# First unit's keys by token tile, Wk on ScalarE's queue, and four pieces of work in other slots, in an attention and expert layer

## The chip, the cores and the metric

The kernel runs on one core of one Trainium2 chip. The metric is the device time of one execution in microseconds (us), as the median of several runs. The profile shows one more execution, recorded by the hardware profiler. The engines are PE (TensorE, matmuls), PEld (its weight loads), DVE (VectorE), ACT (ScalarE), POOL (GpSimd) and SP (SyncE, which issues most of the DMAs). Each takes its instructions in the order in which they were issued to it.

## The reference

The input x has 2 batches of 512 tokens with 512 features, all in float32. The layer is

```python
q, k, v = x @ Wq + bq, x @ Wk + bk, x @ Wv + bv     # 32 query heads, 8 key/value heads, head size 128
q, k = rope(q), rope(k)
ctx = softmax(causal(q k^T / sqrt(128))) v           # four query heads share a key/value head
x = layernorm(x + ctx @ Wo + bo)
z = x @ lora_A[active]^T                             # 4 active experts, rank 8
alpha = softmax(log(prior) + x @ router_W^T + router_b)   # over the active experts
y = x @ W_base^T + b_base + sum_e alpha_e * 2 * (z_e @ lora_B[e]^T)
out = layernorm(x + y)
```

## The kernel before, in words

A unit is one key/value head of one batch: its four query heads against its own keys, 16 units in all. A unit has 16 score blocks ("slots") of 32 queries x 4 heads = 128 rows. The order of all instructions is written out by hand (`tc.manual_schedule()`): a function `slot(T)` issues what belongs to slot T, for T from -8 on, and `put(T, f)` hangs further work at the end of a slot. In slot T, TensorE gets query products, key or value products, output products, the score of block T and the context products of an older part; then ScalarE and VectorE get the exponentials, sums and transposes of blocks T-1 to T-4. A score bank in PSUM is used again two slots later, so the score of block s needs the exponential of block s-2. The probabilities are transposed through VectorE and a round trip over DRAM (`blocks_out`, `blocks_in`, on SP's queue).

**The start.** Lines 193 to 210 issue the loads: ScalarE's queue the three bias loads into `bqk`; SP's queue the four x tiles of batch 0, Wk of the first head (`load_k(0)`, line 198), Wq of two heads, the rope table, Wq of the other two, Wv, the x tiles of batch 1, and more. The DMA semaphores are eight, given out in turn to the DMAs of the two queues; an issue that uses one again waits until the DMA that had it has landed. On TensorE, lines 1048 to 1057 issue three idle matmuls, the transposes of the four tiles (`transpose_token_tile`, four 128x128 transposes into one bank and one copy, alternately on VectorE and ScalarE, line 282), the transpose `tb` of the biases (line 1054), and then the keys of unit 0: four matmuls with 512 columns, one for each 128 features (`k_mm`, line 361). After it stand the query projection of unit 0 (`q_mm`, two heads, a value tile, two heads) with `q_rope`, and `k_rope` with the rope table on VectorE.

**Wo's sums.** Most products use a seven-product scheme for 2x2 blocks. For the output projection, four VectorE operations (`wo_sums`, line 637) form sums of Wo's blocks in `wt` and in Wo itself, once for each set n of Wo. Lines 942 to 945 put them at slots relative to `wo_from(u) = 16 u + 21`. For set 0 they are at slots 21, 22, 22 and 24. The first product that reads `wt` is in slot 23.

**W_base's transposes.** In the last slots, from `T_PROJ = T_END - 19`, W_base is loaded in four chunks (line 1114, on SP's queue) and transposed (`transposed_base`, line 1111): four transposes on TensorE and a copy on ScalarE (line 282) for each chunk, at slots T_PROJ + 4, 6, 8 and 10.

**The end.** After the slots come the last token tiles of the second half by hand (lines 1137 to 1223). The objects are `f0` (tiles of batch 0), `fz = f0[3]`, `fa`, `fb`, `fc` (tiles of batch 1). `logits` and `alphas` (lines 789 to 810) do the routing: two VectorE operations, an exponential on ScalarE, and VectorE operations that end in `zs`; `low_rank` transposes `zs` into `zT` (tile `tz`, line 814, copy line 815); `finish` adds the low-rank product (line 819); `sum` adds x (line 829); `add` is `sum` and the statistics (lines 703, 704); `root` is the root on ScalarE (line 711) and the reciprocal on VectorE (line 714). The exponential and the root need different tables on ScalarE, so that table loads stand between them.

Of the kernel before, what the change touches and what calls it, by code (L numbers as in the profile page):

```python
# [9 lines left out]
F32 = mybir.dt.float32  # L10
# [5 lines left out]
P = 128  # L16
# [3 lines left out]
D = 128  # L20
# [9 lines left out]
def postln_layer_kernel(  # L30
# [33 lines left out]
    nc = tc.nc  # L64
    B, S, HID = x.shape
    NT = B * S // P
    TPB = S // P
    KC = HID // P
# [19 lines left out]
    NSETS = len(sets)  # L88

    def unit(u):  # L90
        return units[u]
# [4 lines left out]
    def set_units(n):  # L96
        return [u for u in range(NU) if set_of(u) == n]
# [8 lines left out]
    ps_q = ctx.enter_context(tc.tile_pool(name="ps_q", bufs=1, space=bass.MemoryType.PSUM))  # L106
    ps_k = ctx.enter_context(tc.tile_pool(name="ps_k", bufs=1, space=bass.MemoryType.PSUM))
    ps_sc = ctx.enter_context(tc.tile_pool(name="ps_sc", bufs=2, space=bass.MemoryType.PSUM))
# [5 lines left out]
    x_sb = const.tile([P, NT, HID], F32, name="x_sb")  # L114
# [3 lines left out]
    NBIAS = H + 2 * G  # L118
    bqkT = const.tile([P, NBIAS], F32, name="bqkT")
# [7 lines left out]
    ident = const.tile([P, P], F32, name="ident")  # L127
# [10 lines left out]
    xT = proj.tile([P, KC, B * S], F32, name="xT")  # L138
# [6 lines left out]
    wqk = {}  # L145
    wos = {}
    wvs = {}

    def load_k(g):
        wk_g = wts.tile([P, KC, D], F32, tag="wk_g", name=f"wk_{g}")  # L150
        nc.sync.dma_start(out=wk_g, in_=Wk[:, ts(g, D)].rearrange("(c p) n -> p c n", p=P))
        wqk["k", g] = wk_g

    def load_q(n, k):
        wq_g = wts.tile([P, KC, 2 * D], F32, tag="wq_g", name=f"wq_{n}_{k}", bufs=3)
        lo = (sets[n] * R + 2 * k) * D
        nc.sync.dma_start(out=wq_g, in_=Wq[:, lo : lo + 2 * D].rearrange("(c p) n -> p c n", p=P))
        wqk["q", n, k] = wq_g
# [11 lines left out]
    def load_x(t, n):  # L170
        nc.sync.dma_start(
            out=x_sb[:, t : t + n, :], in_=xf[t * P : (t + n) * P, :].rearrange("(t p) n -> p t n", p=P))


    for n in range(2):
# [6 lines left out]
        out=tri, in_=tri, pattern=[[-BLK, QB], [-1, BLK]], compare_op=ALU.is_ge,  # L182
# [6 lines left out]
    for z in zt:  # L189
        nc.gpsimd.memset(z, 0.0)  # L190

    bqk = setup.tile([NBIAS, D], F32, name="bqk")
    nc.scalar.dma_start(out=bqk[:H, :], in_=bq.rearrange("(h d) -> h d", d=D))
    nc.scalar.dma_start(out=bqk[H : H + G, :], in_=bk.rearrange("(h d) -> h d", d=D))
    nc.scalar.dma_start(out=bqk[H + G :, :], in_=bv.rearrange("(h d) -> h d", d=D))
    for t in range(TPB):
        load_x(t, 1)
    load_k(0)
    load_q(0, 0)
    nc.sync.dma_start(out=rope_sb, in_=rope[:, 2:4, :])  # L200
    load_q(0, 1)
    load_wv(0)
    load_x(TPB, 2)
    load_x(TPB + 2, 2)
    load_k(1)
    bo_bc = setup.tile([P, HID], F32, name="bo_bc")
    nc.sync.dma_start(out=bo_bc, in_=bo.partition_broadcast(P))
# [66 lines left out]
            gather(b_act[:, a, :], lora_B.rearrange("e (p j) r -> (e p) (j r)", j=BJ), idx["b"][:, a : a + 1])  # L274


    def transpose_token_tile(dst, src, pool, tag, copy):

        tp = pool.tile([P, KC, P], F32, tag=tag, name="tp")
        for c in range(KC):  # L280
            nc.tensor.transpose(tp[:, c, :], src[:, ts(c, P)], ident)  # L281
        copy(dst, tp)

    b_jar = setup.tile([P, BJ, EA, RK], F32, name="b_jar")

# [40 lines left out]
    psq = {}  # L326
    sc = {}
# [27 lines left out]
    in_psum = set()  # L355

    def proj_mm(key, pool, tag, wt, cols, b, c):
        if c == 0:
            psq[key] = pool.tile([P, S], F32, tag=tag, name="pp")
            in_psum.add(key)  # L360
        nc.tensor.matmul(  # L361
            psq[key], lhsT=wt[:, c, cols], rhs=xT[:, c, ts(b, S)], start=(c == 0), stop=(c == KC - 1))
# [22 lines left out]
    def k_mm(u, c):  # L385
        g, b = unit(u)
        proj_mm(("k", u), ps_k, "k", wqk["k", g], slice(0, D), b, c)

    def k_of(u):
        if u not in kT:  # L390
            kT[u] = work.tile([P, UNIT, BLK], F32, tag="kT", name=f"kT_{u}", bufs=5)
        return kT[u]
# [234 lines left out]
    def wo_sums(n, step):  # L627

        if step == 0:
            shape = [P, 3, CH, NHALF]  # L630
            if n == NSETS - 4:
                wt[n] = late["pool"].tile(shape, F32, name="wt_late")
            else:
                wt[n] = wow.tile(shape, F32, tag="wt", name=f"wt_{n}", bufs=1)
        t1, t2, t4 = (wt[n][:, m] for m in range(3))
        b11, b12, b21, b22 = (wo_block(n, c_half, n_half) for c_half in range(2) for n_half in range(2))
        nc.vector.tensor_tensor(
            *((t1, b12, b11), (t2, b22, t1), (b12, b22, b12), (t4, b21, t2))[step], ALU.subtract)
# [104 lines left out]
    class Ffn:  # L743
# [22 lines left out]
        def transpose(self, pool, tag):  # L766
            transpose_token_tile(self.xT, self.x, pool, tag, nc.scalar.copy)
# [107 lines left out]
    def put(slot, f):  # L875
        extra.setdefault(slot, []).append(f)

    copies = (nc.vector.tensor_copy, nc.scalar.copy)
# [39 lines left out]
    for p in range(1, G // VG):  # L918
        at = PERIOD * p
        put(13 if p == 1 else at - PERIOD + 9, lambda p=p: load_k(VG * p))  # L920
        put(37 if p == 1 else at - PERIOD + 13, lambda p=p: load_k(VG * p + 1))
        put(40 if p == 1 else at - 2 * UNIT + 3, lambda p=p: kv_sums("k", p))
        if p > 1:
            put(at - PERIOD + 37, lambda p=p: load_wv(p))
        put(at + (UNIT if p == 1 else 0) + 3, lambda p=p: kv_sums("v", p))
# [10 lines left out]
    def wo_from(u):  # L936
        return UNIT * u + LAG_WO
# [2 lines left out]
        put(wo_from(set_units(n - 2)[-1] + 1) + 1, lambda n=n: load_wo(n))  # L940

    for n in range(NSETS - 2):
        at = {NSETS - 4: (-16, -15, -15, -13), NSETS - 3: (-11, -9, -6, -5)}.get(n, (0, 1, 1, 3))
        for k in range(4):
            put(wo_from(set_units(n)[0]) + at[k], lambda n=n, k=k: wo_sums(n, k))

# [15 lines left out]
    def slot(T):  # L962
# [14 lines left out]
        if 0 < uk < PLAIN_K and l < KC:  # L977
            k_mm(uk, l)
# [66 lines left out]
    spare = ((ps_wo, "wx"), (ps_wo, "wy"), (ps_ctx, "ctx"), (ps_sc, "sc"))  # L1045
# [2 lines left out]
    idle = ps_sc.tile([P, 2 * P], F32, tag="sc", name="idle")  # L1048
    for _ in range(3):
        nc.tensor.matmul(idle, lhsT=maskw[:, :P], rhs=maskw[:, : 2 * P], start=True, stop=True)  # L1050
    for t in range(TPB):
        transpose_token_tile(xT[:, :, ts(t, P)], x_sb[:, t, :], *spare[t], copies[t % 2])
    tb = ps_sc.tile([P, NBIAS], F32, tag="sc", name="tb")
    nc.tensor.transpose(tb, bqk, ident[:NBIAS, :NBIAS])
    nc.vector.tensor_copy(bqkT, tb)
    for c in range(KC):
        k_mm(0, c)
    for part in range(3):
        k_rope(0, part)
    expert_rows()  # L1060
# [1 line left out]
    for r in range(R):  # L1062
        for c in range(KC):
            q_mm(0, r, c, *q_banks[r])
        for part in range(3):
            q_rope(0, r, part)
        if r == 2:
            for t in range(TPB, NT):
                transpose_token_tile(xT[:, :, ts(t, P)], x_sb[:, t, :], *spare[t % 2 + 2], nc.scalar.copy)
        elif r:  # L1070
            v_tile(0, r // 2, *spare[r // 2 * 2])
            v_out(0, r // 2)
# [9 lines left out]
    T_PROJ = T_END - 19  # L1082
# [15 lines left out]
    def tiles(ts_, banks, name):  # L1098
        n = len(ts_)
        norms = Norm(ffn_pool, n, f"a{name}"), Norm(ffn_pool, n, f"f{name}")  # L1100
        return [Ffn(t, bank, *norms, i) for i, (t, bank) in enumerate(zip(ts_, banks))]

    f0 = tiles(range(TPB), ((QX, QY), (QX, QY), (SC, SC), (QX, QY)), "0")
    fa = tiles([TPB + i for i in order[:2]], ((SC, SC), (WX, WY)), "1a")
# [5 lines left out]
    def transposed_base(c):  # L1110
        transpose_token_tile(wbT[:, :, c // 2, ts(c % 2, P)], wb_sb[:, c, :], ps_k, "k", nc.scalar.copy)

    for c in range(OC):
        put(T_PROJ + (0, 1, 4, 5)[c], lambda c=c: nc.sync.dma_start(out=wb_sb[:, c, :], in_=W_base[ts(c, P), :]))
        put(T_PROJ + (4, 6, 8, 10)[c], lambda c=c: transposed_base(c))
    put(A - 5, lambda: f0[0].norm1.newton(0, 2))
    for k, f in enumerate(f0):
        put(A + (-7, -6, 0, 0)[k], f.stats)
# [18 lines left out]
    fz = f0[3]  # L1137
# [17 lines left out]
    fb.centre()  # L1155
    f0[2].norm2.stats(2, f0[2].y)
    f0[0].norm2.root(0, 3)
    for f in f0[:3]:
        f.store()
    for j in range(2):  # L1160
# [2 lines left out]
    for f in fa:  # L1163
        f.transpose(*SC)
    fb.transpose(*CTX)
    fz.logits()
    fz.alphas()
    for r in range(R):
        wo_mm(NP - 1, r)
    wo_out(NP - 1)  # L1170
# [30 lines left out]
    fb.logits()  # L1201
    fb.alphas()
    fa[1].finish()
    fa[1].add()
    fa[1].norm2.sqrt(1, 2)
    for c in range(KC):
        fc.half(0, c)
    fc.half_end(0)
    fb.low_rank()
    fa[1].norm2.invert(1, 2)  # L1210
    fa[1].store()
    fc.half_stats(0)
    for c in range(KC):
# [60 lines left out]
```

## Time and profile before

| | |
|---|---|
| median of three runs | 823.33 us (822.33 to 825.24) |
| profiled execution: time | 822.99 us |
| profiled execution: span of the instructions | 821.2 us |
| busy in the span | PE 810.6, DVE 603.7, ACT 379.2, POOL 320.9 us |
| granted TensorE clock | 0.999 |

The page gives the busy time of each engine, the chain of work that ended last, the groups of instructions by line and the DMA issues. Times in it are counted from the start of the span. A float32 matmul stands in the records as two; PE's ends are modelled, so a stop of TensorE is read from the starts of successive matmuls, and from the release shown in brackets at the end of a row: how long the engine was idle before, and what ended it.

### The profile page before, as it was taken

To read this page: it belongs to the slowest core of one execution; us is meant where nothing else is said; L and a number is where in the kernel's file an instruction comes from. 1 tells how busy PE (TensorE), PEld (TensorE's weight loads), DVE (VectorE), ACT (ScalarE), POOL (GpSimd) and SP (SyncE) were. 2 spreads that over 40 slices of the span, in tenths; PEclk is the share of its full clock that TensorE was granted. 3 is DMA by queue.
4 is the path that set the end of the run, shared out by engine and by line. 5 is a ranking of instruction groups with operands and counts; after the bars stand their busy time and mean duration, and the time that the engine had idled before them with its cause. 6 is when DMAs were issued, how large, how long until landed. Compare 5 with 4: busy or idle time off the path is not lost.

```text
span 821.2 us, 11196 instructions
## 1 busy us (share of the span) xinstructions
PE 810.6 (99%) x3385; PEld 598.5 (73%) x3385; DVE 603.7 (74%) x1972; ACT 379.2 (46%) x1058; POOL 320.9 (39%) x377
## 2 busy tenths in 40 slices
PE   8999999999999999999999999999999999999996
PEld 5567777777777778777777878777777878655565
DVE  4367877677878876787868777787888689974455
ACT  1236453453545554444545444444545454663244
POOL 6464343512543545321453245343464333420033
PEclk9999999999999999999999999999999999999999
DMA  9015636445474637354454627355453726674211
GB/s 306 22 39 148 213 77 174 134 118 163 103 208 107 201 91 218 90 141 156 135 150 126 190 66 224 97 154 180 134 148 96 225 65 183 187 257 142 77 39 65
DMA packets 84415, 116.00 MB, mean 141 GB/s; under 512 B 6525, under 2 KB 64237, under 8 KB 82306
## 3 DMA queue, kind: packets, MB, share of 16 engines
q1 hardware_dynamic: 83682, 114.98, 48.7%
q8 instruction: 27, 0.44, 0.2%
q14 instruction: 34, 0.28, 0.1%
q0 software_dynamic: 448, 0.14, 0.1%
q10 hardware_dynamic: 224, 0.16, 0.1%
HBM read 71.21 MB, written 44.04 MB: 140 GB/s over the span
## 4 chain that ended last, share of the span: by engine, by line
PE 94%; DVE 3%; ACT 1%; DMA 1%; issue 0%; POOL 0%; SPq 0%; DVEq 0%; POOLq 0%
PE pc L608 16%; PE sc L552 14%; PE qx L440 12%; PE wx L440 11%; PE qy L440 9%; PE wy L440 9%; PE pp L361 5%; PE kx L440 4%; PE vx L518 4%; PE py L778 3%; PE po L684 3%; PE pv L344 3%; PE tp L281 1%; PE py L819 1%; DMA x_sb<-_attn_hidden_states_dram 1%; DVE st L703 0%
## 5 line engine op out<-in xcount | busy, mean ns | idle before, releaser
L560 DVE CUSTOM_DVE_ANT_0 sc<-sc,maskw 128x288 f32<-128x288 f32 (+15 forms) x256 | 114.2, 446 | 139.6 <-PE sc L552 138.1
L567 ACT ACTIVATE p<-sc,nmax 128x288 f32<-128x288 f32 (+15 forms) x256 | 124.3, 485 | 200.5 <-DVE nmax L560 179.0
L608 PE MATMUL pc<-pT,v 128*128 128x512 f32 x320 | 165.4, 599 | 0.0
L552 PE MATMUL sc<-kT,qT 128*128 128x160 f32 (+15 forms) x512 | 161.8, 398 | 1.0 <-ACT p L567 1.0
L382 POOL TENSOR_TENSOR qT<-q,t 128x512 f32<-128x512 f32 x56 | 76.5, 1365 | 178.8 <-DVE q L381 176.0
L575 ACT ACTIVATE p<-p,den 128x288 f32<-128x288 f32 (+15 forms) x256 | 133.2, 521 | 0.0
L552 PEld LDWEIGHTS sc<-kT,qT 128*128 128x128 f32 x512 | 96.1, 190 | 23.9 <-issue 9.8
L615 ACT ACTIVATE ctxT<-pc,bqkT 128x512 f32<-128x512 f32 x64 | 44.0, 687 | 118.0 <-PE pc L608 118.0
L427 POOL TENSOR_TENSOR cs<-ctxT 128x256 f32<-128x256 f32 x28 | 22.5, 802 | 157.7 <-PE wy L440 94.5
L583 DVE STREAM_TRANSPOSE zt<-p 128x128 f32<-128x128 f32 (+2 forms) x192 | 81.6, 425 | 0.0
L608 PEld LDWEIGHTS pc<-pT,v 128*128 128x128 f32 x320 | 57.1, 190 | 18.7 <-issue 5.7
L440 PE MATMUL qx<-xs,wq 128*128 128x256 f32 x224 | 58.0, 381 | 0.0
L476 ACT COPY q<-qx 128x256 f32<-128x256 f32 x112 | 41.4, 370 | 35.2 <-PE qx L440 35.1
L440 PEld LDWEIGHTS qx<-xs,wq 128*128 128x128 f32 x224 | 41.4, 190 | 22.2 <-issue 18.4
L440 PE MATMUL wx<-wo,ctxT 128*128 128x256 f32 x224 | 57.6, 379 | 0.0
L585 DVE STREAM_TRANSPOSE zt<-p 128x32 f32<-128x32 f32 (+3 forms) x256 | 57.5, 225 | 0.0
L567 ACT ACTIVATION_READ_ACCUMULATOR p<-sc,nmax 128x1 f32 x256 | 49.8, 195 | 0.0
L440 PEld LDWEIGHTS wx<-wo,ctxT 128*128 128x128 f32 x224 | 42.5, 190 | 7.7 <-issue 1.4
L670 DVE TENSOR_TENSOR x_sb<-wx,x_sb 128x256 f32<-128x256 f32 x112 | 47.0, 420 | 0.0
L374 DVE SCALAR_TENSOR_TENSOR t<-q,bqkT,rope_sb 64x512 f32<-64x512 f32 x56 | 45.6, 815 | 1.5
L377 DVE SCALAR_TENSOR_TENSOR t<-q,bqkT,rope_sb 64x512 f32<-64x512 f32 x56 | 42.7, 762 | 1.3
L571 DVE RECIPROCAL den<-den 128x1 f32<-128x1 f32 x256 | 39.3, 153 | 1.3 <-ACT p L567 1.2
(233 smaller groups left out, 1482.1 us busy)
## 6 DMA issues: line engine op xcount, KB each, us to landing
db<-zt SPq DMA_DIRECT2D x64, 256.0 KB, 4.2
pT<-db SPq DMA_DIRECT2D x16, 1024.0 KB, 4.8
db<-zt SPq DMA_DIRECT2D x64, 192.0 KB, 3.2
pT<-db SPq DMA_DIRECT2D x16, 768.0 KB, 4.5
wq<-in_L_attn_Wq_dram SPq DMA_DIRECT2D x20, 512.0 KB, 5.1
wo<-in_L_attn_Wo_dram SPq DMA_DIRECT2D x10, 1024.0 KB
db<-zt SPq DMA_DIRECT2D x64, 128.0 KB, 2.3
pT<-db SPq DMA_DIRECT2D x16, 512.0 KB, 4.1
```

Of the source, the lines that this page charges most:

```text
L374: nc.vector.scalar_tensor_tensor(t2[lo, :], q[hi, :], b_ap[hi, :], rope_sb[hi, 1, :], ALU.add, ALU.mult)
L382: nc.gpsimd.tensor_tensor(dst, t1[:, :].rearrange("p (n s) -> p n s", s=BLK), t2[:, :].rearrange("p (n s) -> p n s", s=BLK), ALU.add)
L440: nc.tensor.matmul(ps, lhsT=wt[:, c, :], rhs=xt[:, c, :], start=start and c == 0, stop=c == CH - 1, skip_group_check=True)
L552: nc.tensor.matmul(sc[s][:, :w], lhsT=qT[u][:, i * QB + n].rearrange("p r s -> p (r s)"), rhs=kT[u][:].rearrange("p n s -> p (n s)")[:, :w ...
L560: nc.vector.tensor_tensor_reduce(sc[s][:, :w], sc[s][:, :w], maskw[:, S - w :], -SCALE, -MASKED, ALU.add, ALU.min, nmax[s])
L567: nc.scalar.activation(ptile[s][:, :w], sc[s][:, :w], AF.Exp, bias=nmax[s], scale=-1.0, accum_out=rden[s])
L575: nc.scalar.activation(ptile[s][:, :w], ptile[s][:, :w], AF.Copy, scale=rden[s])
L583: nc.vector.transpose(z[:, :, last - i : last, n, :].rearrange("p q j s -> p j q s"), ptile[s][:, : i * P])
L585: nc.vector.transpose(z[:, : n + 1, last, n, :], ptile[s][:, i * P : w])
L608: nc.tensor.matmul(psc[p], lhsT=v_sb[g // VG, b][:, j, ts(g % VG, D)], rhs=pT[p][:, :, ts(j, P)], start=(j == 0), stop=(j == i))
L615: nc.scalar.activation(ctxT[p], psc[p], AF.Identity, bias=bqkT[:, col : col + 1])
L670: nc.vector.tensor_tensor(into, pw[k, bank], into, ALU.add)
```

## The change

Wk's first load moves to ScalarE's queue ahead of the biases. The keys of unit 0 are computed for each token tile of 128 columns (`k_tile`) instead of for 512 columns at once, each tile two steps behind its transposes; the fourth x tile is transposed into two banks with two copies; the biases' transpose moves behind the third tile. Set 0's four Wo sums go to slots 16, 17, 18 and 19. W_base's first and last transposes go one slot earlier. At the end `fz`'s routing is issued before the last context, and `fa[1]`'s statistics and root after `fb`'s copy of `zT`.

```diff
-    def load_k(g):
+    def load_k(g, queue=nc.sync):
...
-        nc.sync.dma_start(out=wk_g, in_=Wk[:, ts(g, D)].rearrange("(c p) n -> p c n", p=P))
+        queue.dma_start(out=wk_g, in_=Wk[:, ts(g, D)].rearrange("(c p) n -> p c n", p=P))
...
+    load_k(0, nc.scalar)
     bqk = setup.tile([NBIAS, D], F32, name="bqk")
...
-    load_k(0)
     load_q(0, 0)
...
-    def transpose_token_tile(dst, src, pool, tag, copy):
+    def transpose_token_tile(dst, src, pool, tag, copy, chunks=range(KC)):
-        tp = pool.tile([P, KC, P], F32, tag=tag, name="tp")
-        for c in range(KC):
-            nc.tensor.transpose(tp[:, c, :], src[:, ts(c, P)], ident)
-        copy(dst, tp)
+        tp = pool.tile([P, len(chunks), P], F32, tag=tag, name="tp")
+        for n, c in enumerate(chunks):
+            nc.tensor.transpose(tp[:, n, :], src[:, ts(c, P)], ident)
+        copy(dst[:, chunks[0] : chunks[-1] + 1, :], tp)
...
+    def k_tile(u, t, c):
+        g, b = unit(u)
+        key = "k", u
+        if t == c == 0:
+            psq[key] = ps_k.tile([P, S], F32, tag="k", name="pp")
+            in_psum.add(key)
+        nc.tensor.matmul(
+            psq[key][:, ts(t, P)], lhsT=wqk["k", g][:, c, :], rhs=xT[:, c, ts(b * TPB + t, P)],
+            start=(t == c == 0), stop=(c == KC - 1), skip_group_check=True)
...
-        at = {NSETS - 4: (-16, -15, -15, -13), NSETS - 3: (-11, -9, -6, -5)}.get(n, (0, 1, 1, 3))
+        at = {0: (-5, -4, -3, -2), NSETS - 4: (-16, -15, -15, -13), NSETS - 3: (-11, -9, -6, -5)}.get(n, (0, 1, 1, 3))
...
     for t in range(TPB):
-        transpose_token_tile(xT[:, :, ts(t, P)], x_sb[:, t, :], *spare[t], copies[t % 2])
-    tb = ps_sc.tile([P, NBIAS], F32, tag="sc", name="tb")
-    nc.tensor.transpose(tb, bqk, ident[:NBIAS, :NBIAS])
-    nc.vector.tensor_copy(bqkT, tb)
-    for c in range(KC):
-        k_mm(0, c)
+        x_to = xT[:, :, ts(t, P)], x_sb[:, t, :]
+        if t > 1:
+            for c in range(KC):
+                k_tile(0, t - 2, c)
+        if t < TPB - 1:
+            transpose_token_tile(*x_to, *spare[t], copies[t % 2])
+        else:
+            for n, bank in enumerate((spare[t], (ps_q, "qx"))):
+                transpose_token_tile(*x_to, *bank, copies[n], range(2 * n, 2 * n + 2))
+        if t == 2:
+            tb = ps_sc.tile([P, NBIAS], F32, tag="sc", name="tb")
+            nc.tensor.transpose(tb, bqk, ident[:NBIAS, :NBIAS])
+            nc.vector.tensor_copy(bqkT, tb)
+    for t in range(TPB - 2, TPB):
+        for c in range(KC):
+            k_tile(0, t, c)
...
-        put(T_PROJ + (4, 6, 8, 10)[c], lambda c=c: transposed_base(c))
+        put(T_PROJ + (3, 6, 8, 9)[c], lambda c=c: transposed_base(c))
...
     f0[0].norm2.root(0, 3)
+    fz.logits()
+    fz.alphas()
     for f in f0[:3]:
         f.store()
...
     fb.transpose(*CTX)
-    fz.logits()
-    fz.alphas()
...
     fa[1].finish()
-    fa[1].add()
-    fa[1].norm2.sqrt(1, 2)
+    fa[1].sum()
...
     fb.low_rank()
-    fa[1].norm2.invert(1, 2)
+    fa[1].norm2.stats(1, fa[1].y)
+    fa[1].norm2.root(1, 2)
     fa[1].store()
```

## The prediction

> **What bounds the kernel now.** I read the page first (busy time, chain of work that ended last), then the busy times by stage, then the places at which TensorE stops: the start, about 102 us, about 720 us and the end. Page and stages:
>
> ```profile
> PE 810.6 (99%) x3385; PEld 598.5 (73%) x3385; DVE 603.7 (74%) x1972; ACT 379.2 (46%) x1058; POOL 320.9 (39%) x377
> PEclk9999999999999999999999999999999999999999
> PE 94%; DVE 3%; ACT 1%; DMA 1%; issue 0%; POOL 0%; SPq 0%; DVEq 0%; POOLq 0%
> ...
> 0.00:8.38 8.38, 5.57 (x23) 4.09 (x24) 2.14 (x5) 2.46 (x3) 7.60 (x20) 1.00 0.75 235
> 102.00:717.00 615.00, 615.00 (x2651) 471.34 (x2652) 483.27 (x1574) 297.73 (x854) 248.84 (x281) 1.00 0.51 145
> 717.00:722.00 5.00, 4.03 (x17) 2.36 (x16) 4.03 (x18) 3.63 (x10) 2.45 (x12) 1.00 0.58 152
> ```
>
> TensorE (PE) is the bound at full clock: between 102 and 717 us it is busy in every one of 615.00 us. Matmul starts follow each other at 0.43 us per recorded 512 columns, so little but more TensorE work, or less standing still, moves the end. Three stretches have holes; the start and the 720 us stretch read so in order of time:
>
> ```profile
> 0.74 1.89 SPq L171 DMA_DIRECT2D x_sb<-_attn_hidden_states_dram  x4
> 2.67 0.45 SPq L151 DMA_DIRECT2D wk<-in_L_attn_Wk_dram  x1
> 3.43 0.37 SPq L157 DMA_DIRECT2D wq<-in_L_attn_Wq_dram  x1
> 5.79 0.66 PE L281 MATMUL tp<-ident,x_sb 128*128 128x128 f32 x4 [0.54 <-DMA x_sb<-_attn_hidden_states_dram]
> 7.05 0.66 PE L281 MATMUL tp<-ident,x_sb 128*128 128x128 f32 x4 [0.60 <-DMA x_sb<-_attn_hidden_states_dram]
> 8.38 3.70 PE L361 MATMUL pp<-xT,wk 128*128 128x512 f32 x8 [0.49 <-ACT xT L282]
> ...
> 101.33 0.59 PE L552 MATMUL sc<-kT,qT 128*128 128x256 f32 x2
> 101.98 1.13 PE L440 MATMUL qy<-xT,wq 128*128 128x256 f32 x4
> ...
> 721.30 0.91 PE L552 MATMUL sc<-kT,qT 128*128 128x384 f32 x2 [0.97 <-ACT p L567]
> ...
> 792.98 0.28 PE L814 MATMUL tz<-ident,zs 128*32 128x128 f32 x1 [0.22 <-DVE zs L805]
> ...
> 812.68 1.13 PE L819 MATMUL py<-bmT,zT 128*128 128x256 f32 x4 [0.51 <-DVE zT L815]
> ```
>
> To see: the key projection cannot start before the fourth x tile has landed (7.05) and been copied (8.38); one score at 721.30 waits for ScalarE, with its own sequence 1.13 us late; at the end two small waits remain.
>
> **Part 1, the start.** Removed: four 128x512 key matmuls at 8.38, 3.44 us until 11.82. Added: sixteen of 128 columns, four per x tile. The nearest row, eight 128x128 records at 0.89 (vx, L518), gives 4 x 0.89 = 3.56, so 0.12 us more work, but three quarters of it can be done while x arrives. The last tile's copy is split over VectorE and ScalarE (about 0.4 us each where one copy took 0.59).
>
> What it costs is in the queues. Wk goes from the fifth place on SP's queue to the first on ScalarE's, ahead of the three bias loads; the table load behind it (2.10 to 3.38) starts some 0.45 us later, and hides, because ScalarE's first copy is at 5.29. The bytes are not free: an x packet (2 KB) took 84 ns, a Wk packet (512 B) 27 ns, on 16 engines, so an x tile is 128 x 84 / 16 = 0.67 us and Wk is 512 x 27 / 16 = 0.86. Tiles three and four therefore land up to 0.86 later, near 6.65 and 7.9.
>
> When Wk lands decides the part, because TensorE runs in order: behind the first key tile, which waits for Wk, stand the third tile's transposes, the bias transpose, the second key tile and the fourth's transposes. The trace's one case of two such queues at work together, the 16 KB of bq at 2.47 to 2.76, shows ScalarE's packets slipping between SP's, but it has only two per engine and does not tell the turn. [...] By turns of single descriptors, 32 against 32, Wk ends with the fourth tile, at 7.9. I take 5.3, and 4.3 to 7.9 as ends.
>
> With 5.3: key tile 1 at 5.35 to 6.24; third transposes 6.65 to 7.08; bias transpose to 7.25 (bq, bk, bv come right behind Wk); key tile 2 to 8.15; fourth transposes to 8.60; key tile 3 to 9.47 (its copy, 0.69 on VectorE, is done by about 8.0); key tile 4 to 10.35. Gain 11.82 - 10.35 = 1.5. With 4.3 the fourth tile alone sets it: 7.9 + 0.43 + 2 x 0.89 = 10.1, gain 1.7, and 2.1 if that tile lands at 7.5. With 7.9: 7.9 + 4 x 0.89 + 2 x 0.43 + 0.15 = 12.5, a loss of 0.7.
>
> One more wait: DMA semaphores are reused every eighth transfer. Before, Wq's issue waited for bq, "SPq L157 <- DMA bqk" 0.3 us; now that slot is Wk's, so Wq's issue, and rope, Wq's second half, Wv and the later x behind it on SP, wait for Wk. With 5.3, Wq starts to move 1.38 after its issue (as x did: 0.74 to 2.12), at about 6.7, when the rings are still full of x; no bytes are lost, Wq lands at about 9.3 as before, and the query matmuls can start at 10.35. The key rope on VectorE waits for rope_sb (10.9) rather than for TensorE (12.12), and the query bank is free at about 17.6, before its next use at 10.35 + 6.88 + 1.73 = 19.0. So all of it is carried on: **1.5, ends -0.7 and +2.1**.
>
> **Part 2, Wo's first sums five to one slots earlier.** The same four VectorE operations (0.69, 0.68, 1.76, 0.69, line 637). At 102 us they made the queue late: the sum q (L480) came at 101.52 and TensorE lost 0.22 + 0.11 us. In the new slots (85 to 94 us) VectorE has idle stretches of 1.56 at 82.8 and 1.69 at 89.1; the score of 96 columns would be masked about 0.6 late, the one of 160 about 0.8 late, and the next need, the qy product at 96.64 that reads what L480 leaves, has 1.1 of slack. Covered, **+0.33**; if a sum again takes 1.7 beside GpSimd, that product waits up to 1.0. Range -0.7 to +0.33.
>
> **Part 3, W_base's first and last transposes a slot earlier.** Same 2 x 0.43 on TensorE and 2 x 0.59 on ScalarE. Before, ScalarE stood 0.88 us until 718.96 for the first transposes, then did copy 0.48, ctxT 0.59, p 0.60, and only then the exponential (720.63) for which the score of 721.30 waited. Moved: transposes 715.91 to 716.34, copy 716.6, p 717.1, exponential 717.65 (0.16 late), ctxT 718.85 (bound by its own matmul), p 719.44, exponential 720.04, so 0.6 earlier: **+0.6**, ends 0 and 1.1. The first W_base chunk (256 KB, issued 711.73) lands by about 714.8, so it is not awaited. The last move finds ScalarE 1 us later at 732.6, with TensorE's need at 735.07: nothing.
>
> **Part 4, the end.** The routing of the fourth tile goes ahead of ctxT on ScalarE: table load 786.09 to 787.37, exponential to 787.8, just ahead of ctxT (787.92), where it was idle for 1.85. The transposed zs is then long ready at 792.60, and the 0.38 wait before 792.98 goes; all that follows comes from TensorE and moves with it. The copy zT ahead of the statistics brings the matmul of 812.68 down to the end of the one before it, but VectorE's own queue is then the limit: statistics 0.2 later, root, reciprocal, half statistics, and the next sum, at 813.41 before, could start at 813.5. So 0.38 - 0.08 = **+0.3**, ends 0 and 0.5.
>
> **Sum.** 1.5 + 0.33 + 0.6 + 0.3 = 2.7 us. The profiled execution took 822.99 (span 821.2 and 1.8 around it), 0.3 under the median of 823.33; it becomes 820.3, and the median 820.6. About 0.3% (2.5 us) is what a measurement of this kernel can tell from no change, so the forecast stands at its edge.
>
> **The rivals.**
> - *The wait only changes its name.* Wk lands at 7.0 to 7.9, keys end at 11.6 to 12.5. For: the bytes needed before the last key matmul are the same in both orders, and engines with two rings may take turns finely. Against: the bq packets were not held back. Gain of part 1 between +0.25 and -0.7, total 0.5 to 1.5: 821.8 to 822.8. Chance 0.2.
> - *The moved slots don't pay.* VectorE's late queue of part 2 and ScalarE's waits of part 3 reappear at the next score, since both engines have in-order queues of 0.6 us pieces there. Then parts 1 and 4 alone: 1.8 us, 821.5. Chance 0.12.
> - *Slower.* In the start, ScalarE's ring is served after SP's whole run of x, and one engine is slow as in this trace (a packet of 1.16 at 4.88). Each 1 us by which Wk lands after 7.25 costs 1 us of the start; past 8.5 it eats the 1.2 of the other parts. At 9.5 the kernel takes 824.4. Against: bq's first packet came 0.35 after x's. Chance 0.08.
>
> **How the numbers follow.** 0.6 for the forecast (its own range 819.6 to 821.6, from parts 1 and 3). Faster by over 0.3% needs less than 820.86, some four fifths of the forecast's case and a little of the others: 0.5. Slower by over 0.3% is the far end of the last rival: 0.06. The rest, 0.44, is within. The range runs from the best ends (2.1, 0.33, 1.0, 0.4: 819.4) to past the first two rivals, with the runs' own spread (822.33 to 825.24): 819.3 to 823.4.
>
> **What would show it.** Right: first key matmul at 5 to 6 us, first wq matmul near 10.4, no hole over 0.2 at about 100 us, the hole before the score of 384 columns at about 0.5, and tz straight after the po matmuls. Wrong: a wait for Wk longer than until 7, a hole at a qy matmul in slot 22, ScalarE's ctxT at the end later than its matmul, or a sum at the end that waits for VectorE.

## The result, and the profile after

The changed kernel takes 821.19 us (median of 19 runs, 820.47 to 823.88), the kernel before in runs on the same chip 823.13 (19 runs, 822.33 to 826.35). The ratio is 0.9973, with a 95% interval of 0.9964 to 0.9983, so about 2.2 us (1.4 to 3.0) are gained; the medians differ by 1.9. A second series on another chip gave 821.19 (15 runs) against 822.80: 0.9981 (0.9973 to 0.9989), 1.6 us. The profiled execution went from 822.99 to 820.47, its span from 821.2 to 818.7. The forecast was 820.6, 2.7 us less than before; it was right in direction and within its range, and its 2.7 us stand beside 2.5 in the profile. That the sum comes so near is in part luck: parts 1 and 2 brought 0.6 us less than forecast, part 4 0.3 more.

The page of the changed kernel, busy times and chain of work:

```profile
PE 810.3 (99%) x3409; PEld 600.7 (73%) x3409; DVE 602.6 (74%) x1973; ACT 378.5 (46%) x1058; POOL 321.3 (39%) x377
PEclk9999999999999999999999999999999999999999
PE 97%; ACT 1%; DVE 1%; DMA 1%; issue 0%; SPq 0%
```

TensorE's busy time is the same to 0.3 us (810.6 before), at the same full clock. Of the 2.5 us by which the span is shorter, 2.2 came out of time in which it stood still (10.6 us before, 8.4 now). The start, in TensorE's groups of the changed kernel (start, busy time, what it is; in brackets the idle time ahead of it and what ended that):

```profile
5.39 0.66 PE L281 MATMUL tp<-ident,x_sb 128*128 128x128 f32 x4 [0.36 <-DMA x_sb<-_attn_hidden_states_dram]
5.88 1.09 PE L396 MATMUL pp<-xT,wk 128*128 128x128 f32 x8
6.81 0.60 PE L281 MATMUL tp<-ident,x_sb 128*128 128x128 f32 x4
...
7.53 1.16 PE L396 MATMUL pp<-xT,wk 128*128 128x128 f32 x8
8.52 0.60 PE L281 MATMUL tp<-ident,x_sb 128*128 128x128 f32 x4
8.96 1.95 PE L396 MATMUL pp<-xT,wk 128*128 128x128 f32 x16
10.75 3.60 PE L361 MATMUL pp<-xT,wq 128*128 128x512 f32 x8
```

From 5.88 on TensorE no longer stops: transposes and key matmuls alternate, and the query begins at 10.75, where it began at 11.92. The DMA issues on the two queues at the start:

```profile
0.74 1.82 SPq L171 DMA_DIRECT2D x_sb<-_attn_hidden_states_dram  x4
4.67 0.38 SPq L157 DMA_DIRECT2D wq<-in_L_attn_Wq_dram  x1
0.73 0.47 ACTq L151 DMA_DIRECT2D wk<-in_L_attn_Wk_dram  x1
```

Wq's issue, which now waits for Wk's slot (2.1 us by the profile, where it waited 0.3 for that of bq), went out at 4.67 and not at 3.43: that is when Wk had landed, 0.6 us earlier than the 5.3 of the forecast. The other places of the changed kernel, first near 95 us (TensorE, then VectorE):

```profile
94.61 1.02 PE L619 MATMUL pc<-pT,v 128*128 128x512 f32 x2
95.60 1.13 PE L451 MATMUL qy<-xT,ws 128*128 128x256 f32 x4
```

```profile
91.93 1.10 DVE L648 TENSOR_TENSOR wt<-wo,wt 128x512 f32<-128x512 f32 x1
95.13 0.42 DVE L491 TENSOR_TENSOR q<-qy,q 128x256 f32<-128x256 f32 x1
```

The holes here are small and carry no bracket; they show in the distances. Where nothing waits, the group behind two 512-column records starts 0.86 after them (95.52 to 96.38 in the kernel with these sums one slot earlier, below); here it is 0.99 (94.61 to 95.60), so 0.13 is lost ahead of the product qy. Another 0.11 is lost inside it: it is busy for 1.13, and four such records take 1.03 elsewhere. Then 720 us and the end:

```profile
719.39 0.91 PE L563 MATMUL sc<-kT,qT 128*128 128x384 f32 x2 [0.35 <-ACT p L578]
...
787.31 3.60 PE L695 MATMUL po<-wo,ctxT 128*128 128x512 f32 x8
790.74 0.27 PE L825 MATMUL tz<-ident,zs 128*32 128x128 f32 x1
...
808.78 0.27 PE L825 MATMUL tz<-ident,zs 128*32 128x128 f32 x1
808.89 1.03 PE L847 MATMUL ph<-wbT,x1T 128*128 128x256 f32 x4
809.76 1.03 PE L830 MATMUL py<-bmT,zT 128*128 128x256 f32 x4
```

The score of 384 columns waits 0.35 in its bracket where it waited 0.97 (by the starts of the matmuls the holes are 0.61 and 1.13); tz stands right behind the po matmuls, and the low-rank product (809.76) right behind the half before it. Adding up from one landmark to the next, before against after:

| stretch | landmark | gain in the profile | forecast |
|---|---|---|---|
| part 1 | first query matmul 11.92 to 10.75 | 1.17 | 1.5 |
| part 2 | holes 0.33 near 102, now 0.13 + 0.11 near 95 | 0.09 | 0.33 |
| part 3 | 1.13 ahead of the score and 0.11 inside the product before it, now 0.61 ahead of the score | 0.6 | 0.6 |
| part 4 | 0.38 ahead of the fourth tile's tz; then from the last tz to the last reciprocal 5.97, now 5.73 | 0.62 | 0.3 |
| sum | | 2.5 | 2.7 |

The sum meets the difference of the two profiled executions, 822.99 - 820.47 = 2.52.

### The profile page after: what moved, and what is told of

It is laid out like the page before. It is cut to its first block, busy times and chain, and to the rows that moved or that the text cites. A ratio compares the mean times of both kernels' runs of the same rounds, so it can differ in the third digit from the quotient of the medians.

```text
span 818.7 us, 11244 instructions
## 1 busy us (share of the span) xinstructions
PE 810.3 (99%) x3409; PEld 600.7 (73%) x3409; DVE 602.6 (74%) x1973; ACT 378.5 (46%) x1058; POOL 321.3 (39%) x377
## 4 chain that ended last, share of the span: by engine, by line
PE 97%; ACT 1%; DVE 1%; DMA 1%; issue 0%; SPq 0%
PE pc L619 17%; PE sc L563 15%; PE qx L451 12%; PE wx L451 12%; PE qy L451 9%; PE wy L451 9%; PE pp L361 5%; PE kx L451 4%; PE vx L529 4%; PE po L695 3%; PE py L789 3%; PE pv L344 3%; PE tp L281 1%; PE py L830 1%; DMA x_sb<-_attn_hidden_states_dram 1%; PE pp L396 0%
## 5 line engine op out<-in xcount | busy, mean ns | idle before, releaser
L381 DVE SCALAR_TENSOR_TENSOR q<-q,bqkT,rope_sb 128x512 f32<-128x512 f32 x56 | 40.1, 715 | 0.0
```

## The experiments

Each part was put alone into the kernel before, part 1 was divided, one part was moved further, and the whole was run without part 1. All were timed beside the kernel before on the same chip.

### Part 1 alone, and its two halves

**Part 1 alone** is the kernel before with the start of the changed one and nothing else.

> Part 1 alone on the kernel before (Wk first on ScalarE's queue, keys by tile). The theory, from the changed kernel's profile, in which the first query matmul starts at 10.75 us against 11.92: the span falls by about 1.2 us and nothing of it is given back later, so ratio about 0.9985. The rival, that part of it is given back at a later wait: a smaller loss of span than the shift at the query matmul.

Measured: 822.09 against 822.72 us, ratio 0.9990 (0.9981 to 0.9998). The first query matmul is at 11.13; the holes near 102 and 720 us are as before. The start comes earlier by 0.8 in the profile, and the time by 0.8 by the ratio (0.2 to 1.6; the medians differ by 0.6): part 1 pays on its own, less than 1.5. From the first query matmul to the end of the span it takes 809.23 here and 809.27 in the kernel before, so that nothing of the earlier start is given back.

That the query came 0.38 later than in the changed kernel, with the same start, has a cause in TensorE's clock:

```profile
5.26 1.12 PE L281 MATMUL tp<-ident,x_sb 128*128 128x128 f32 x4 [0.29 <-DMA x_sb<-_attn_hidden_states_dram]
6.17 1.18 PE L396 MATMUL pp<-xT,wk 128*128 128x128 f32 x8
```

The second tile's four transposes take 0.91 to the next group (5.26 to 6.17), in the changed kernel 0.49 (5.39 to 5.88). In the profiles the transposes follow each other at 0.21 us before the trace's first record of the granted clock, and at 0.11 after it. That record stands at 5.04 us in the changed kernel and at 6.42 here; over the 14 profiles it lies between 4.04 and 7.28. So TensorE starts at about half its later speed (0.21 for 0.11), and when this ends differs between executions. The profile's clock column does not show it: it gives 1.00 for the time before the first record too.

**Keys tile by tile, but Wk in its old place** behind x on SP's queue (the edit against part 1 alone):

```diff
-    load_k(0, nc.scalar)
     bqk = setup.tile([NBIAS, D], F32, name="bqk")
...
     for t in range(TPB):
         load_x(t, 1)
+    load_k(0)
     load_q(0, 0)
```

> Part 1 with keys by tile, but Wk in its old place on SP's queue behind the four x tiles. If the early Wk is what makes the part pay: Wk lands near 7.8 us, the first key tile waits for it and with it everything behind it on TensorE (third and fourth transposes, bias transpose, other key tiles, 4.9 us in the changed kernel), the first query matmul starts near 12.7, 0.8 us later than before, ratio about 1.001. Rival, that splitting the keys is what pays and the queue is indifferent: first query matmul at about 10.8.

Measured: 825.15 against the kernel before at a ratio of 1.0030 (1.0018 to 1.0042): 2.5 us slower, with the first query matmul at 14.39. TensorE's groups of this kernel:

```profile
8.14 2.05 PE L396 MATMUL pp<-xT,wk 128*128 128x128 f32 x8 [3.06 <-DMA wk<-in_L_attn_Wk_dram]
9.98 1.06 PE L281 MATMUL tp<-ident,x_sb 128*128 128x128 f32 x4
...
11.17 1.16 PE L396 MATMUL pp<-xT,wk 128*128 128x128 f32 x8
12.16 0.60 PE L281 MATMUL tp<-ident,x_sb 128*128 128x128 f32 x4
```

The order alone loses: on TensorE the first key tile stands in front of the third tile's transposes, Wk behind all of x comes at 8.14, and those transposes start behind the key tile at 9.98, where they started at 5.79 in the kernel before. The loss is larger than the delay explains, though. The eight key records that follow take 1.84 us to the next group (8.14 to 9.98), later 0.99 (11.17 to 12.16), and four transposes 0.99 (9.98 to 10.97), later 0.44. The busy times by stretch of this kernel show why (the stretch, its length, then busy time and count of TensorE's matmuls, its weight loads, VectorE, ScalarE and GpSimd; then the granted clock of TensorE, the DMA share and GB/s):

```profile
4.18:7.59 3.41, 0.91 (x8) 0.67 (x6) 0.69 (x1) 0.58 (x1) 3.40 (x5) 1.00 0.94 300
8.00:9.00 1.00, 0.86 (x4) 0.89 (x5) 0.00 (x0) 0.00 (x0) 1.00 (x3) 0.50 1.07 409
11.00:11.50 0.50, 0.50 (x5) 0.45 (x5) 0.42 (x1) 0.00 (x0) 0.00 (x0) 1.00 0.87 287
```

The granted clock fell to half at 7.6 us, while TensorE stood still, and came back at 11.0, after 3.4 us. So the wait cost its own 3 us and then 1.4 more at half clock (0.85 + 0.55). The page's clock row does not show it: a digit there stands for a mean over 20 us. The 3.41 us before the fall were not idle throughout: TensorE worked in them until about 5.1, for 0.91 us.

**Wk first on ScalarE's queue, keys whole as before** (the edit against the kernel before; `load_k` takes the queue as in the change):

```diff
+    load_k(0, nc.scalar)
     bqk = setup.tile([NBIAS, D], F32, name="bqk")
...
         load_x(t, 1)
-    load_k(0)
     load_q(0, 0)
```

> Wk first on ScalarE's queue, but the keys in four matmuls of 512 columns after all four tiles, as before. The prediction's term: Wk's 0.86 us on the DMA engines delays the fourth x tile by up to 0.86, the first key matmul moves from 8.38 to about 9.2 and the span grows by about 0.8. Rival, read from the changed kernel, where the last x packet ended at 6.61 as it did before: no delay, first key matmul near 8.4, ratio 1.000.

Measured: 822.76 us, ratio 1.0003 (0.9995 to 1.0011). TensorE's groups of this kernel:

```profile
5.41 0.66 PE L281 MATMUL tp<-ident,x_sb 128*128 128x128 f32 x4 [0.76 <-DMA x_sb<-_attn_hidden_states_dram]
6.21 1.30 PE L281 MATMUL tp<-ident,x_sb 128*128 128x128 f32 x8 [0.15 <-DMA x_sb<-_attn_hidden_states_dram]
...
8.19 3.70 PE L361 MATMUL pp<-xT,wk 128*128 128x512 f32 x8 [0.49 <-ACT xT L282]
```

The second tile is late (5.41), but the third and fourth are not: the key matmuls start at 8.19, where they started at 8.38. The forecast's delay of 0.86 to those two tiles does not exist. The trace's packets say why. In the changed kernel the 512 packets of Wk ran from 2.80 to about 4.2 us; when they ended, 196 of x's 512 packets had started, 128 to a tile. So Wk went mostly ahead of the second tile. The last x packet ended 4.49 after the first started (6.27 and 1.78), in the kernel before 4.48 (6.57 and 2.09); over the five profiles with Wk in front it is 4.37 to 4.65, over the seven with the old start 3.91 to 5.50. Between 4.0 and 4.5 the DMA engines moved 147 GB/s in the kernel before and 427 in the changed one: Wk in part filled a gap.

So neither half pays alone: one loses 2.5 us, the other is worth nothing that can be told, and together they give the gain of part 1.

### Part 2

**Part 2 alone:**

```diff
-        at = {NSETS - 4: (-16, -15, -15, -13), NSETS - 3: (-11, -9, -6, -5)}.get(n, (0, 1, 1, 3))
+        at = {0: (-5, -4, -3, -2), NSETS - 4: (-16, -15, -15, -13), NSETS - 3: (-11, -9, -6, -5)}.get(n, (0, 1, 1, 3))
```

> Wo's first sums in slots 16 to 19 alone. The prediction: no hole near 95 us, the hole of 0.33 near 102 gone, span 0.33 us shorter. The rival, read from the changed kernel: VectorE's queue is late at the sum q of slot 21, because two of the four sums take 1.1 us beside GpSimd's sums; TensorE loses about 0.24 us at the qy product of slot 22 and gains 0.33 later, net 0.1 us. Both are under what the times can tell; the holes in the profile decide.

Measured: 822.74 us, ratio 1.0004 (0.9997 to 1.0010). The holes are those of the changed kernel. VectorE's groups:

```profile
89.03 1.12 DVE L637 TENSOR_TENSOR wo<-wo 128x512 f32<-128x512 f32 x1
...
91.10 0.98 DVE L377 SCALAR_TENSOR_TENSOR t<-q,bqkT,rope_sb 64x512 f32<-64x512 f32 x1
92.12 1.10 DVE L637 TENSOR_TENSOR wt<-wo,wt 128x512 f32<-128x512 f32 x1
...
95.31 0.42 DVE L480 TENSOR_TENSOR q<-qy,q 128x256 f32<-128x256 f32 x1
```

Two of the four sums take 1.1 where 0.69 was counted, and the rope's second operation 0.98 where it took 0.75 before; its first one is shorter, 0.82 after 1.10. GpSimd is at work beside them from 86.9 to 92.7, and two of its own operations grew too, from 0.73 in the kernel before to 1.06 and 1.17: side by side, operations of both engines took longer. VectorE thus has 0.8 more to do than was counted. The sum q ahead of the product qy starts at 95.31, 0.35 before the 95.66 at which that product was due (0.86 after the matmuls at 94.80); in the kernel before it started at 95.09, 1.55 before the product at 96.64. It is 1.2 later, and the forecast's slack was 1.1.

**The four sums one slot earlier still**, (-6, -5, -4, -3) in the line above:

> Wo's first sums alone, in slots 15 to 18, one slot earlier than in the change. If the late sum q of slot 21 is what took part 2's gain (0.24 of 0.33 us), VectorE now has the idle stretch of about 1.7 us before the score of 96 columns to catch up: no hole near 95 us, none near 102 us, span 0.33 us less than with the old slots at the same start. If the hole comes from elsewhere (GpSimd's sums alone), it stays at about 95 us.

Measured: 822.48 us, ratio 0.9997 (0.9989 to 1.0005). TensorE's groups of this kernel:

```profile
95.52 1.02 PE L608 MATMUL pc<-pT,v 128*128 128x512 f32 x2
96.38 1.03 PE L440 MATMUL qy<-xT,ws 128*128 128x256 f32 x4
...
101.50 1.03 PE L440 MATMUL qy<-xT,wq 128*128 128x256 f32 x4
```

Neither the hole near 95 nor the one near 102 is left. So the place of part 2, not its idea, kept it from its 0.33. From the first query matmul to the end of the span it takes 808.95, 0.32 less than before (809.27); part 2 alone takes 809.19. A third of a microsecond can be read from the trace; the times do not tell it.

### Part 3

**The first transposes of W_base alone, one slot earlier:**

```diff
-        put(T_PROJ + (4, 6, 8, 10)[c], lambda c=c: transposed_base(c))
+        put(T_PROJ + (3, 6, 8, 10)[c], lambda c=c: transposed_base(c))
```

> Only W_base's first transposes a slot earlier, the last ones left. Theory: the hole before the score of 384 columns falls from 1.13 to 0.6 us and nothing else changes, so all of part 3 (0.5 to 0.6 us, ratio 0.9993) is in the first move. Rival, that the last move carries some of it: less than 0.5 gained here.

Measured: 822.91 us, ratio 1.0005 (0.9997 to 1.0013). TensorE's groups, and the chain of work that leads to the last of them:

```profile
721.02 0.91 PE L552 MATMUL sc<-kT,qT 128*128 128x384 f32 x2 [0.39 <-ACT p L567]
...
724.62 1.12 PE L608 MATMUL pc<-pT,v 128*128 128x512 f32 x2 [0.69 <-DMA pT<-db]
```

```profile
715.80 4.27 DMA db<-zt
...
720.14 4.44 DMA pT<-db
724.62 1.12 PE pc L608 x2
```

The hole before the score shrank from 1.13 to 0.61, and the 0.11 inside the product ahead of it is gone, as expected 0.6 in all; 3.6 us later a new hole of 0.86 opened. The chain tells what it is: a block of probabilities is written out (4.27), read back transposed (4.44), and only then multiplied. This pair of transfers starts at 715.80, ahead of the hole, and does not get shorter when the hole does. In the kernel before, the readback was issued at 719.49; at the 4.50 from issue to landing in this trace (720.08 to 724.58) it landed near 724.0, an estimate, and the matmul that needs it started at 724.05. By this estimate the old hole was hiding a chain that had next to nothing to spare.

How late the pair ends differs between executions. The hole ahead of that pc matmul was 0.80 in the kernel without part 1, 0.22 in the second profile of the changed kernel, 0 in the first, and 0.41 in a kernel that has the old place of the transposes (the copy alone, below). Part 3 thus exposes this wait where the transfers come late, and the profile that shows its full 0.6 was one in which they came in time.

### Part 4

**The routing of the fourth tile alone:**

```diff
     f0[0].norm2.root(0, 3)
+    fz.logits()
+    fz.alphas()
     for f in f0[:3]:
...
     fb.transpose(*CTX)
-    fz.logits()
-    fz.alphas()
```

> Only the fourth tile's routing ahead of the last context on ScalarE. Theory: the hole of 0.38 us before the transpose of zs after the last output products goes, ctxT is not later, and everything after moves by 0.38 us; the hole before the last low-rank product (0.68) stays. Ratio 0.9995.

Measured: 822.50 us, ratio 1.0000 (0.9990 to 1.0010). The 0.38 ahead of tz is gone; the hole ahead of the last low-rank product is there as before.

**The copy ahead of the statistics alone:**

```diff
-    fa[1].add()
-    fa[1].norm2.sqrt(1, 2)
+    fa[1].sum()
...
     fb.low_rank()
-    fa[1].norm2.invert(1, 2)
+    fa[1].norm2.stats(1, fa[1].y)
+    fa[1].norm2.root(1, 2)
```

> Only the copy of zT ahead of the second tile's statistics at the end. The prediction: TensorE's hole of 0.68 us goes, but the next sum on VectorE starts 0.08 us later, so the end is 0.1 us later. Rival, from the changed kernel, where the part from that sum to the end moved 0.24 us more than the matmuls before it: the end is 0.2 us earlier.

Measured: 822.84 us, ratio 1.0000 (0.9991 to 1.0009). The profiled execution took 825.29 and began its query 2 us late, which belongs to the start (below), so only distances within the end are used. From tz of the last tile to the last reciprocal it takes 5.72 (813.60 to 819.32); the kernel before takes 5.97 (811.03 to 817.00), the routing alone 5.97, the changed kernel 5.73. The copy is worth +0.24, where the forecast had -0.08. VectorE's groups of the changed kernel show where that comes from:

```profile
809.18 0.27 DVE L826 COPY zT<-tz 32x128 f32<-32x128 f32 x1
809.38 0.67 DVE L714 BATCH_NORM_STATS2 st<-y 128x6 f32<-128x512 f32 x1
...
810.71 0.41 DVE L857 BATCH_NORM_STATS2 st<-ph 128x6 f32<-128x256 f32 x1
811.04 0.74 DVE L840 TENSOR_TENSOR y<-py,x_sb 128x256 f32<-128x256 f32 x2
```

The sum starts 2.26 after tz (808.78), before 2.38; and it runs 0.74 where it ran 0.86, because both halves of the product are ready when it starts. The 0.51 that stood between half statistics and sum before (812.90 to 813.41) was the late product's doing; VectorE itself is ready for the next operation after 0.33.

### The whole again, without part 1, and two further versions

**Parts 2, 3 and 4 without part 1**, beside the changed kernel:

> Parts 2, 3 and 4 without part 1. The holes that they close add up to 0.1 + 0.6 + 0.6 = 1.3 us, so ratio about 0.9985, and the difference to the whole change is what part 1 is worth as a median over its varying start. Rival, that part 1 is all of the gain in the times: ratio 1.000.

> The changed kernel once more, beside the three that follow. The theory that the gain is 0.5 to 1 us at the start and 1.3 us in later holes: ratio near 0.9975, first query matmul between 10.7 and 11.2 us.

Measured: without part 1 822.58 us, ratio 0.9994 (0.9983 to 1.0005); the changed kernel 821.19, ratio 0.9981 (0.9973 to 0.9989). The start carries most of what can be measured. From the first query matmul to the end of the span the kernel before takes 809.27, the kernel without part 1 808.79, the changed kernel 807.94 and 808.20. In the profiles with the old order of the start, the first query matmul lies at 11.92, 10.96, 11.65, 12.24, 11.83, 12.04 and once at 14.00; with the new one at 10.75, 11.13, 10.64 and 10.83. The 14.00 is that of the copy alone; TensorE's groups of it, and its busy times by stretch (columns as above):

```profile
6.99 1.31 PE L281 MATMUL tp<-ident,x_sb 128*128 128x128 f32 x8 [1.43 <-DMA x_sb<-_attn_hidden_states_dram]
...
8.98 5.18 PE L361 MATMUL pp<-xT,wk 128*128 128x512 f32 x8 [0.49 <-ACT xT L282]
14.00 4.46 PE L361 MATMUL pp<-xT,wq 128*128 128x512 f32 x10
```

```profile
5.16:8.57 3.41, 1.90 (x13) 1.13 (x11) 1.27 (x3) 0.81 (x2) 3.40 (x5) 1.00 1.04 339
9.00:10.00 1.00, 1.00 (x2) 0.48 (x3) 0.00 (x0) 0.00 (x0) 0.99 (x4) 0.50 0.97 350
12.00:13.00 1.00, 1.00 (x3) 0.42 (x3) 0.00 (x0) 0.00 (x0) 0.00 (x0) 1.00 1.10 366
```

Here the third tile came late (1.43 of waiting), the clock fell to half at 8.6 and came back at 12.0, again 3.4 us, and the key projection took 5.0 instead of 3.5. The clock's records tell what went before: counted from its first record, its changes come at whole multiples of 3.41 us. In the two profiles that lost it, it fell 3.41 us after that record and came back 6.82 after it (4.18, 7.59 and 11.0; 5.16, 8.57 and 12.0); in the kernel before and in the changed one it changes only once, near the end of the span, after 815.79 and 812.37 us, which are 239 and 238 times 3.413. In the two that lost it, TensorE was busy for 0.91 and 1.90 of the 3.41 us before the fall; in the other twelve the first such stretch at full clock holds 2.20 or more. The nearest on this side, and one with the new start:

```profile
4.22:7.63 3.41, 2.20 (x17) 1.56 (x15) 1.35 (x2) 0.59 (x1) 3.40 (x5) 1.00 0.99 284
```

```profile
4.47:7.88 3.41, 2.88 (x24) 2.42 (x23) 1.23 (x2) 0.58 (x1) 3.40 (x5) 1.00 0.98 324
```

The first is of the routing alone, the second of the changed kernel's second profile. With the old start this stretch holds 1.90 to 2.93 us of work, with the new one 2.88 to 3.41. So the old start, with its holes, can lose the clock, and no profile of the new one lost it.

The times agree in part: of all executions of kernels with the old start (the kernel before among them, the two that took part 1 apart left out) 22 of 242 were more than 2 us above the median of their kernel on that chip, and with the new start 1 of 80. The clock is not the cause of all of them. For 17 of the 22 the mean granted clock is on record, and 3.41 us at half clock take 0.002 off it. Eight show 0.995 to 0.997, which fits a loss (the profile of the copy alone has 0.996). Nine show 0.999: these lost nothing once the clock had come up, and were 2.8 to 3.7 us late all the same. What held them up is not shown.

By the ratios part 1 alone gives 0.8 us, the other three 0.5, all together 1.6 and 2.2. The intervals of the two single ones reach to 1.6 and 1.4 us, so their sum is no contradiction, but it cannot be confirmed in the times.

**Two further versions.** The first has the sums of part 2 one slot earlier and, at the end, one square root for the last two full tiles:

```diff
-    fa[0].norm2.stats(0, fa[0].y)
-    fa[0].norm2.sqrt(0, 1)
...
-    fa[0].norm2.invert(0, 1)
-    fa[0].store()
...
+    for f in fa:
+        f.norm2.stats(f.i, f.y)
+    fa[0].norm2.sqrt(0, 2)
```

> The changed kernel with Wo's first sums one slot earlier still and, at the end, the third tile's routing and both tiles' statistics so ordered that one root serves two tiles and two table loads fall away. Theory: no hole at 95 us (0.24 less), and the sum after the last low-rank product bound by TensorE and no longer by VectorE behind the table load (0.5 less): 0.7 us less than the changed kernel, ratio about 0.9967. Rival, that the stores on GpSimd, which now start together, hold the last stores back: end not earlier.

Measured: 821.28 us, ratio 0.9981 (0.9972 to 0.9989). From the last pair of matmuls to the last square root it takes 1.75, where the changed kernel of the same series takes 2.28; but this execution lost 1.13 us to the transposed probabilities near 722. The second version also puts the second x tile first on ScalarE's queue, with Wk behind it and one bias load moved to SP's queue, and divides the first tile's copy:

```diff
+    load_x(1, 1, nc.scalar)
     load_k(0, nc.scalar)
...
-    for t in range(TPB):
+    for t in (0, 2, 3):
         load_x(t, 1)
```

> best_a with the second x tile first on ScalarE's queue, Wk after it, one bias load on SP's, and the first tile's copy split in two as well. If in the changed kernel the run of Wk's packets between the first and the second x tile is what makes TensorE wait until 5.4 us, the second tile is transposed at about 4.5 us, key tile 1 starts near 5.3, TensorE then runs without a stop and the first query matmul starts near 10.3, 0.4 to 0.8 us earlier: ratio about 0.996. Rival: Wk now lands after 5.5 us and the start is the same or later.

Measured: 821.01 us, ratio 0.9976 (0.9968 to 0.9983). The second tile comes earlier, Wk's packets later (4.16 to 5.34), and the query starts at 10.85, no earlier than before that edit (10.83). In this execution the clock came up only at 5.95, and the first two tiles' transposes ran without a wait at 0.21 each until 5.94; what the earlier tile is worth with the clock up sooner, this profile does not tell. Neither version can be told from the changed kernel: their intervals overlap nearly whole. At the end the earlier last store (issued at 815.03, 815.65 in the changed kernel) ended no sooner (span 819.0 and 818.8). GpSimd now normalises two tiles back to back and ends at 814.26 instead of 813.12, so a store of 256 KB falls together with the last ones. That this is the cause is read from the trace and was not tried.

## Why the prediction was right, and which steps were not

**What bounds the kernel** was right: 0.3 us of difference in TensorE's busy time, and 2.2 us less of standing still.

**Part 1**, mechanism right, size 0.3 too large (1.17 for 1.5). The step that failed is *"Tiles three and four therefore land up to 0.86 later"*. Wk's packets went mostly ahead of the second x tile, partly into time in which the DMA engines had been half idle (a share of 0.49 between 4.0 and 4.5 in the kernel before), and the last x packet kept its distance from the first. What was late was the second tile (transposed from 5.39, from 4.66 before). Its transposes stand ahead of the first key tile, which so began at 5.88 and not at 5.35, although Wk had landed 0.6 before the forecast's 5.3. From there TensorE worked without a wait and took 4.87 to the query, where the forecast had 5.00 with waits in it: 10.75 and not 10.35. (The forecast also put the old query at 11.82; the trace has 11.92.)

No run shows the 5.3 from which this part was added up, nor the 4.3 at its better end: they were the author's estimate of when Wk lands, and in what turn the DMA engines serve two queues is not shown, as the trace does not tell which engine moved a packet. What the runs showed in their place is that Wk's 512 packets ran from 2.80 to about 4.2, that 196 of x's 512 packets had started by then, and that Wk had landed at 4.67. The rival in which the wait only changes its name is out for Wk on ScalarE's queue; Wk on SP's queue shows what it would have cost.

**Part 2**, wrong in size (0.09 for 0.33), by the bound that the step named: *"the qy product at 96.64 that reads what L480 leaves, has 1.1 of slack"*, and *"if a sum again takes 1.7 beside GpSimd, that product waits"*. Two sums of 1.1 and a rope operation of 0.98 were enough. The step that failed is the count of 0.69 for every sum. The rival that the moved slots don't pay was right for this part, and one slot earlier both holes are gone.

**Part 3**, right at its own place (0.6, in the kernel with that edit alone too). What it left out is what stands behind the hole: the round trip of the probabilities through DRAM. The gain holds when the transfers come in time, and is handed on to the next wait when they don't. The forecast followed ScalarE's waits only, not the chain that the pc matmul at 724.05 waits for.

**Part 4**, half of the size missing (0.62 for 0.3). The term 0.38 was exact. *"Could start at 813.5"* was wrong: the half statistics hold VectorE for 0.33 and not 0.5, and the sum itself became shorter by 0.12, which the step did not consider. Both were in the profile before: the second record shows as 0.86 against 0.74 for the sum of the tile ahead of it.

**The slower rival**, in which ScalarE's queue (its "ring" in the forecast) is served after SP's run of x, did not come, as Wk landed at 4.67, far from the 7.25 from which it costs. With Wk on SP's queue and used from 8.14, the start lost 2.5 us. The rival's line of one for one past 7.25 would give 0.9: it did not count the half clock behind the wait (1.4).

**The signs.** Those of being right came: the first key matmul at 5.88, the query at 10.75 for 10.4, the score's hole at 0.61, tz straight behind the po matmuls. Of those of being wrong two came in small: a hole at the qy product of slot 22 (0.13 + 0.11), and a sum at the end that waits for VectorE (it starts at 811.04, and its product ends by 810.79), earlier than before all the same. The lower end of the range was summed with 1.0 and 0.4 where parts 3 and 4 name 1.1 and 0.5; nothing hangs on it.

## What to carry to other kernels

Work that arrives in pieces can be used in pieces only if what it is multiplied with is there first; the reordering and the earlier load gave a loss and nothing apart, and about 1 us together. A start without holes kept TensorE's clock in all five of its profiles; one with holes lost it in one of seven. Before a hole is closed, look at the next semaphore behind it: a round trip through memory that just fits under the hole takes the gain back (0.6 closed and 0.86 opened in part 3 alone). Where a slot for a side operation is chosen, count it at the price that it has beside its neighbour engine, 1.1 and not 0.69 here. To compare executions whose starts differ, measure from a landmark behind the start: from the first query matmul to the end, four kernels that differ only in their start agree to 0.04 us (809.23 to 809.27).

## What the runs showed of the hardware

- The clock of TensorE fell to half for 3.4 us where TensorE had been busy for 0.91 and 1.90 of the 3.41 us before (two profiles, at 7.6 and 8.6 us). It stayed in the other twelve, where the first 3.41 us of its records held 2.20 or more. It shows in stretches of one or two microseconds, not in the page's row of 20. A wait of 3.06 us cost 1.4 more in this way.
- At the start TensorE ran at about half speed (transposes at 0.21 and not 0.11) until a time between 4.04 and 7.28 us, with no record of it in the clock column.
- With two queues at work at the start, 512 packets of 512 bytes went through in some 1.4 us (2.80 to 4.2), mostly ahead of the second of four tiles of 128 packets of 2 KB that had been issued at about the same time: 196 of the 512 packets of 2 KB had started by then.
- VectorE and GpSimd took longer side by side: sums of 0.69 took 1.1 beside GpSimd, and GpSimd's of 0.73 took 1.06 and 1.17.
- Transfers with the same code differ between executions: the last x packet ended 3.9 to 5.5 us after the first started in seven profiles of the old start, and the matmul behind the readback near 722 us waited from 0 to 1.13.
